# A selective scan over whole images, its input in PSUM, a multiply on GpSimd, and an output projection that moves into the next layer

## The chip, the cores and the metric

The kernel runs on one core of a Trainium2 chip. A core has four engines that matter here, each with its own queue of instructions: PE (TensorE, matrix products), DVE (VectorE, elementwise work and the scan), ACT (ScalarE, functions such as exp) and POOL (GpSimd). POOL and SP (SyncE) also issue most of the transfers between the chip's memory (DRAM) and the core's on-chip memories: SBUF, with 128 partitions, and PSUM, the small memory into which PE writes its sums. PSUM is used here as eight banks of 128 partitions x 512 floats.

The metric is the device time of one execution in microseconds (us). Everything is fp32.

## The reference

Eight images of 384 channels and 32x32 positions go through four layers. The change concerns the first and the head of the second.

Layer 0 norms an image (RMS over channels), flattens it to 1024 positions and runs a Mamba block forwards and backwards over them with the same weights; a gated 3x3 depthwise convolution is added. The core of it, for one direction:

```
u, z   = split(x_flat @ in_proj.T)                  # 384 channels each
u      = silu(causal depthwise conv of 4 taps(u))
dt,B,C = split(u @ x_proj.T)                        # 24, 16 and 16 columns
delta  = softplus(dt @ dt_proj.T + bias)            # one per channel and position
h[l]   = exp(delta[l] * A) * h[l-1] + delta[l] * u[l] * B[l]   # 16 states a channel
y[l]   = sum over the 16 states of h[l] * C[l]  + D * u[l]
out    = (y * silu(z)) @ out_proj.T
```

The layer's result is x + 0.5 * (0.25 * (out forwards + out backwards) + sigmoid(conv3x3(xn)) * xn).

Layer 1 is a 1x1 convolution, a 3x3 depthwise one and another 1x1 (with batch norms), a residual, linear attention with 8 heads, a layer norm and an MLP of 4x384 with an exact GELU. Layer 2 is a sum of seven depthwise convolutions with batch norms, which the kernel merges into one 13x13; layer 3 is a 1x1 convolution with a residual and a second 13x13 depthwise convolution with GELU.

## The kernel before

Layers 0 and 1 run together in `_layers01`, image by image; layers 2 and 3 follow when all images are through. For image b there are three strands of work, written as Python generators:

- `front(b)`, layer 0 up to the scan's inputs. It works by halves of 512 positions and by chunks of 128 channels, and leaves in DRAM delta (`dl_d`, one for each direction), delta*u (`v_d`), u of both directions added (`ud_d`), silu(z) (`z_d`), and the rows B and C (`bc_d`); x plus the local branch goes to `x1_d`. Its last step for a half is `deltas`: on DVE an add (L689), a multiply (L690) for each direction and an add of the two u, then the writes, which POOL issues.
- `scan(b)`, the scan and the output projection.
- `layer1(b)`, the second layer, which reads `x1_d`.

The main loop (L1067-1104) goes through the 48 units of scan(b). After each unit it advances the other strands, front(b+1) and layer1(b-1), so that their steps are spread over the units by their weights (90 and 310). A scheduler of the framework then fixes, at build time, the order of the instructions on each engine; so the order in which they run is near to the written one, but not the same. Buffers come from pools: a tile that has no free buffer in its pool makes the instruction that fills it wait.

A unit of the scan covers one direction d, one half h, one chunk c of 128 channels and one round r of 4 of the 16 states. The 128 partitions hold 32 channels times 4 states; the four groups j of 32 channels lie side by side, so a tile is 128 x (4 x 512). Delta and delta*u are loaded from DRAM with each channel's row given to four partitions (`dlt`, `vt`), B and C with each state's row given to 32 partitions (`bct`, two loads for each round); SP issues these. A unit is then:

- ACT: four exponentials (L775) make `da`, each with the scale -A of its partitions.
- DVE: one multiply by B over all four groups (L788) makes `du`. Then, for the unit before this one (`pend`), the multiply by C (L712), and then this unit's scan (L795 forwards, L798 backwards). One instruction scans all four groups: they are joined by one extra column each (`SEG` = 513), which restarts the recurrence with zero (a memset, L787) or with the first half's last state (`carry`, copies L785 and L802).
- PE: four matmuls (L714) with `selt`, a 128x32 matrix that sums the four states, add the product into `acc`, a PSUM bank for 128 channels x 512 positions, over the four rounds. `acc` starts as D*u through a diagonal matrix (`dgd`, direction 0) or as the forward result through the identity (direction 1).

After round 3 the forward sum is copied out by ACT (L723) and kept in `yf_d`; the backward sum is multiplied by silu(z) (`zr`) on DVE into `g` (L728). At the last chunk of a half the output projection follows at once: three output blocks of three matmuls each, `x1` is loaded again (`fr`), one DVE instruction adds (L737), and POOL issues the write to `x1_d`.

PSUM's banks: two for `acc`, three for the tag `mm` (`psum`) and three for `mo` (`long_psum`), which belongs to the MLP's long sums.

## Time and profile before

| | |
|---|---|
| device time, median of 3 runs | 5962.13 us (5957.54 to 5968.36) |
| time of the profiled execution | 5912.56 us |
| its span in the profile | 5910.8 us |
| mean granted clock of PE | 0.879 of full speed |
| busy: PE / DVE / ACT / POOL | 80% / 69% / 48% / 20% |
| matmuls / DVE instructions | 19550 / 2815 |

Where the time lies, by the start of each image's first B and C load (times in us from the start of the span, then the busy time of PE and DVE within):

| stretch | us | PE | DVE |
|---|---|---|---|
| scan of image 0 | 230-689 | 259 | 434 |
| image 1 | 689-1294 | 457 | 495 |
| image 2 | 1294-1941 | 496 | 497 |
| image 3 | 1941-2558 | 494 | 485 |
| image 4 | 2558-3114 | 478 | 491 |
| image 5 | 3114-3664 | 476 | 491 |
| image 6 | 3664-4215 | 468 | 476 |
| image 7 | 4215-4775 | 463 | 513 |
| rest of the last second layer | 4775-5050 | 235 | 23 |
| layers 2 and 3 | 5050-5911 | 809 | 136 |

How to read the profile's lines. A group of instructions is shown as line, engine, operation, output<-inputs by the program's names, partitions x elements, xcount, then the total busy time in us and the mean length of one in ns; behind the second bar stands the idle time of the engine just before them and what ended most of it. "SPq" and "POOLq" are the transfers that SP and POOL issue. A line of waits reads "PE acc L714 <- DVE du L712": PE's instruction of L714 waited for DVE's of L712; the numbers are us in total, times, and the longest. A line of the timeline gives start and length in us, engine, line, operation, tiles.

### The profile page before, as it was taken

To read this page: it belongs to the slowest core of one execution; us is meant where nothing else is said; L and a number is where in the kernel's file an instruction comes from. 1 tells how busy PE (TensorE), PEld (TensorE's weight loads), DVE (VectorE), ACT (ScalarE), POOL (GpSimd) and SP (SyncE) were. 2 spreads that over 40 slices of the span, in tenths; PEclk is the share of its full clock that TensorE was granted. 3 is DMA by queue.
4 is the path that set the end of the run, shared out by engine and by line. 5 is a ranking of instruction groups with operands and counts; after the bars stand their busy time and mean duration, and the time that the engine had idled before them with its cause. 6 is when DMAs were issued, how large, how long until landed. Compare 5 with 4: busy or idle time off the path is not lost.

```text
span 5910.8 us, 54428 instructions
## 1 busy us (share of the span) xinstructions
PE 4739.8 (80%) x19550; PEld 2105.2 (36%) x19550; DVE 4066.5 (69%) x2815; ACT 2825.7 (48%) x3934; POOL 1208.1 (20%) x2006
## 2 busy tenths in 40 slices
PE   3555557995788777978987988699878879899999
PEld 1121113331333223323332333243223324498498
DVE  0499999668955898588999899879979931011211
ACT  1544635574446635574676567557835523000211
POOL 5311121222112211221122122212210010110133
PEclk8676678997889878989998999899989979999999
DMA  8655574677546754675466457736663541366576
GB/s 278 199 171 183 169 229 153 194 202 200 188 145 187 221 184 139 168 209 161 158 209 207 149 183 199 202 124 200 178 175 114 142 102 37 86 170 161 188 168 149
DMA packets 417253, 1016.66 MB, mean 172 GB/s; under 512 B 61256, under 2 KB 111640, under 8 KB 416984
## 3 DMA queue, kind: packets, MB, share of 16 engines
q0 software_dynamic: 176576, 635.46, 37.1%
q1 hardware_dynamic: 210704, 354.31, 19.6%
q10 hardware_dynamic: 29704, 23.41, 1.5%
q8 instruction: 155, 2.54, 0.2%
q14 instruction: 114, 0.93, 0.1%
HBM read 768.58 MB, written 288.36 MB: 179 GB/s over the span
## 4 chain that ended last, share of the span: by engine, by line
PE 30%; DVE 26%; issue 21%; DMA 11%; ACT 6%; POOL 4%; SPq 1%; POOLq 0%; DVEq 0%; ACTq 0%
DVE du L798 7%; DVE du L788 7%; DVE du L795 6%; PE cv_a L316 5%; PE mo L1043 3%; DVE du L712 3%; PE in L508 3%; PE mf L508 3%; PE q L508 2%; PE acc L714 2%; DMA vr<-v_d 2%; POOL out L368 1%; ACT da L775 1%; DMA x_d<-fr 1%; PE dw L517 1%
## 5 line engine op out<-in xcount | busy, mean ns | idle before, releaser
L775 ACT ACTIVATE da<-dlt,neg_a 128x512 f32<-128x512 f32 x1536 | 1008.3, 713 | 987.3 <-DVE du L795 512.1
L788 DVE TENSOR_TENSOR du<-vr,bct 128x2048 f32<-128x2048 f32 x384 | 874.1, 2282 | 33.0 <-DMA vr<-v_d 27.1
L712 DVE TENSOR_TENSOR du<-du,bct 128x2048 f32<-128x2048 f32 x384 | 877.0, 2285 | 13.9 <-issue 10.4
L714 PE MATMUL acc<-du,selt 128*32 128x512 f32 x3072 | 596.8, 690 | 350.0 <-DVE du L712 335.1
L795 DVE TENSOR_TENSOR_SCAN du<-da,du 128x2052 f32<-128x2052 f32 x192 | 848.2, 4425 | 13.9 <-ACT da L775 10.6
L798 DVE TENSOR_TENSOR_SCAN du<-da,du 128x2052 f32<-128x2052 f32 x192 | 848.4, 4424 | 10.4 <-ACT da L775 7.2
L1043 PE MATMUL mo<-hm,w 128*128 128x512 f32 x1152 | 568.0, 635 | 84.3 <-ACT hm L1041 76.8
L508 PE MATMUL mf<-ln,w 128*128 128x512 f32 x1152 | 551.7, 618 | 24.2 <-DMA w<-w_d 22.4
L1043 PEld LDWEIGHTS mo<-hm,w 128*128 128x128 f32 x1152 | 221.4, 201 | 424.6 <-issue 254.8
L714 PEld LDWEIGHTS acc<-du,selt 128*32 128x32 f32 x3072 | 101.4, 115 | 682.2 <-DVE du L712 434.9
L508 PEld LDWEIGHTS mf<-ln,w 128*128 128x128 f32 x1152 | 215.7, 195 | 350.1 <-issue 327.4
L517 PE MATMUL dw<-dw_i,t3b 96*32 96x512 f32 x1152 | 250.1, 737 | 83.4 <-DMA dw_i<-h_d 71.5
L316 PE MATMUL cv_b<-xt_b,toep 128*64 128x256 f32 x2688 | 305.4, 389 | 14.0 <-DVE xt_b L298 14.0
L316 PE MATMUL cv_a<-xt_a,toep 128*64 128x256 f32 x2688 | 304.4, 388 | 8.8 <-DVE xt_a L298 8.8
L316 PEld LDWEIGHTS cv_b<-xt_b,toep 128*64 128x64 f32 x2688 | 282.7, 199 | 37.0 <-issue 16.7
L508 PE MATMUL in<-xn,win 128*128 128x512 f32 x576 | 291.1, 643 | 3.3 <-DVE biasf L845 2.5
L316 PEld LDWEIGHTS cv_a<-xt_a,toep 128*64 128x64 f32 x2688 | 282.5, 199 | 30.4 <-issue 10.0
L775 ACT ACT_TABLE_LOAD x213 | 273.3, 1283 | 37.0 <-DVE du L798 33.3
L517 PE MATMUL lc<-lc_i,t 96*32 96x512 f32 x1152 | 186.1, 662 | 62.3 <-DMA lc_i<-xn_d 60.1
L1041 ACT ACTIVATE hm<-mf,biasf 128x512 f32<-128x512 f32 x192 | 130.1, 687 | 197.7 <-PE mf L508 195.8
L298 DVE COPY xt_b<-xt_b 64x2480 f32<-64x2480 f32 x24 | 39.0, 1624 | 262.8 <-DMA xt_b<-xp_d 262.8
L508 PE MATMUL h<-xx,c 128*128 128x512 f32 x288 | 150.2, 681 | 67.9 <-DMA xx<-x_d 54.6
(221 smaller groups left out, 6209.3 us busy)
## 6 DMA issues: line engine op xcount, KB each, us to landing
dlt<-dl_d SPq DMA_DIRECT2D x384, 256.0 KB, 5.8
vr<-v_d SPq DMA_DIRECT2D x384, 256.0 KB, 4.9
bct<-bc_d SPq DMA_DIRECT2D x256, 256.0 KB, 4.3
ut<-u_d POOLq DMA_DIRECT2D x192, 257.5 KB, 4.6
lc_i<-xn_d POOLq DMA_DIRECT2D x192, 228.8 KB, 4.6
dw_i<-h_d POOLq DMA_DIRECT2D x192, 228.8 KB, 5.2
tp_d<-g_d POOLq DMA_DIRECT2D x64, 672.0 KB, 7.9
w<-w_d POOLq DMA_DIRECT2D x64, 576.0 KB, 5.2
```

Of the source, the lines that this page charges most:

```text
L316: nc.tensor.matmul(ps[2 * H * e : 2 * H * (e + 1), 0:BW], tp[:, 2 * (g % (GB // 2)) + e, :, :, t].rearrange("p c j -> p (c j)"), rhs, star ...
L368: nc.gpsimd.dma_start(ov[g * P : (g + 1) * P], ot.rearrange("p (b w) -> p b w", w=W))
L508: nc.tensor.matmul(ps, w[:, k, m * P : (m + 1) * P], rhs[k] if isinstance(rhs, list) else rhs[:, k, :], start=(k == 0), stop=(k == NC - 1),)
L517: nc.tensor.matmul(ps[32 * j : 32 * j + 32, :], lhs(j, i), rhs(j, i), start=(i == 0), stop=(i == taps - 1), skip_group_check=True,)
L712: nc.vector.tensor_mul(dv, dv, cct[:, 1:2, :].to_broadcast([P, 4, HALF]))
L714: nc.tensor.matmul(acc[32 * j : 32 * j + 32, :], selt, dv[:, j, :], start=False, stop=(r == NR - 1), skip_group_check=True,)
L775: nc.scalar.activation(da[:, SEG * j + 1 : SEG * (j + 1)], dlt[:, j, :], AF.Exp, scale=neg_a[:, 4 * c + j, r : r + 1],)
L788: nc.vector.tensor_mul(flat(1)[:, :, 0:HALF], vt, bct[r][:, 0:1, :].to_broadcast([P, 4, HALF]))
L795: nc.vector.tensor_tensor_scan(du[:, s], da[:, s], du[:, s], 0.0, ALU.mult, ALU.add)
L798: nc.vector.tensor_tensor_scan(du[:, s][:, ::-1], da[:, s][:, ::-1], du[:, s][:, ::-1], 0.0, ALU.mult, ALU.add)
L1041: nc.scalar.activation(hm, ps, AF.Gelu, bias=biasf[:, NC * i + f, :])
L1043: nc.tensor.matmul(acc[m], wb[:, f, m * P : (m + 1) * P], hm, start=(i == 0 and f == 0), stop=(i == FF // C - 1 and f == NC - 1),)
```

## The change

The scan goes over whole images. A unit is now one direction d, one block u of 64 channels (there are six) and one round r; its two groups j of 32 channels are tiles of their own, 128 x 1024 each, all positions in one piece. So there are still 48 units an image, with the same elements each, but no halves, no joined segments and no carry.

- The exponentials are two of 1024 in place of four of 512. The multiply by B and the scan are two each, one per group. The multiply by B writes `du` into PSUM (one buffer of two banks), the scan reads it there and writes its states `h` to SBUF (five buffers `hs`).
- The multiply by C of group 0 is made by GpSimd, right behind that group's scan; that of group 1 stays on DVE and comes, as before, behind the next unit's first multiply by B.
- PE sums as before with four matmuls of 512 a unit. `acc` holds 64 channels x 2 halves. The add of D*u is no matmul with a diagonal matrix any more: `deltas` multiplies u by D on ACT before it is written, and both directions now add through the identity (L714 of the changed kernel), behind the first round's sums.
- `yf_d` takes the forward sums in the layout of `acc`. The backward sums times silu(z) go to a new DRAM tensor `g_d` rather than to an SBUF tile.
- The output projection leaves `scan` and stands at the head of `layer1(b)`: it loads x1 and g for a half, makes the nine matmuls, and adds in place; the second layer's 1x1 convolution then reads that tile. x1 isn't written a second time. The weight of layer1 in the main loop goes from 310 to 325.
- PSUM: `acc` one bank, `du` two, `mm` two, `mo` three. The second layer's steps up to the layer norm take `mo` in place of `mm`.

In the changed kernel the exponential is L762, the multiply by B L764, the deferred multiply by C L766, the scan L769, GpSimd's multiply L773, the sums over states L708; delta's steps are L681 and L682; the loads of delta and delta*u L750, of B and C L739.

The diff, cut to its core; in `scan`, longer runs of removed lines, which stand in the listing of the kernel before, are left out:

```diff
-SEG = HALF + 1
+NU = C // 64
+N_REP, N_DA, N_HS = 6, 3, 5
...
-        accp = ctx.enter_context(tc.tile_pool(name="acc0", bufs=2, space=PSUM))
+        accp = ctx.enter_context(tc.tile_pool(name="acc0", bufs=1, space=PSUM))
...
-        yf_d = scratch([B, C, L], "yf_d")
+        yf_d = scratch([B, NU, P, HALF], "yf_d")
+        g_d = scratch([B, C, L], "g_d")
...
-        for c in range(NC):
-            nc.gpsimd.tensor_scalar_mul(dgd[:, c, :], ident, vec("D", c))
...
-            return psp.tile([P, HALF], FP, tag="mm", name=name)
+            return psp.tile([P, HALF], FP, tag="mm", name=name, bufs=2)
...
-                        nc.gpsimd.dma_start(udv[b][:, c, bass.ts(h, HALF)], ucs[0][:, c, :])
+                        ud = t2(f"ud_{b}_{h}_{c}")
+                        nc.scalar.activation(ud, ucs[0][:, c, :], AF.Copy, scale=vec("D", c))
+                        nc.gpsimd.dma_start(udv[b][:, c, bass.ts(h, HALF)], ud)
...
             pend = None
...
+            units = [(d, u, r) for d in range(2) for u in range(NU) for r in range(NR)]
+
+            def halves(t_d, u):
+
+                return bass.AP(
+                    t_d.tensor, t_d[b, 64 * u, 0].offset, [[HALF, 2], [L, 64], [1, HALF]]
+                )
             def product(un):
...
+                d, u, r, hs, acc, y0, zt = un
+                for e in range(2):
+                    for j in range(2):
+                        nc.tensor.matmul(
+                            acc[64 * e + 32 * j : 64 * e + 32 * j + 32, :], selt,
+                            hs[j][:, bass.ts(e, HALF)],
+                            start=(r == 0), stop=(r == NR - 1), skip_group_check=True,
+                        )
+                if r == 0:
                     nc.tensor.matmul(
-                        acc[32 * j : 32 * j + 32, :], selt, dv[:, j, :],
-                        start=False, stop=(r == NR - 1), skip_group_check=True,
+                        acc, ident, y0, start=False, stop=False,
+                        skip_group_check=True,
                     )
-                cols = bass.ts(h, HALF)
                 if r < NR - 1:
                     return
                 if d == 0:
-                    yt = s2(f"yt_{b}_{h}_{c}")
+                    yt = s2(f"yt_{b}_{u}")
                     nc.scalar.copy(yt, acc)
...
+                    nc.gpsimd.dma_start(yf_d[b, u], yt)
+                else:
+                    nc.vector.tensor_mul(zt, acc, zt)
+                    nc.gpsimd.dma_start(halves(g_d, u), zt)
+
+            bct = dlt = vt = acc = y0 = zt = None
+            for d, u, r in units:
+                if u == 0 and r == 0:
                     bct = []
                     for e in range(NR):
-                        t = sp.tile([P, 2, HALF], FP, tag="bct", name=f"bct_{b}_{d}_{h}_{e}", bufs=4)
+                        t = sp.tile([P, 2, L], FP, tag="bct", name=f"bct_{b}_{d}_{e}", bufs=4)
                         for o in range(2):
                             src = bass.AP(
-                                bc_d.tensor, bc_d[b, d, o * NST + 4 * e, h * HALF].offset,
-                                [[0, 32], [L, 4], [1, HALF]],
+                                bc_d.tensor, bc_d[b, d, o * NST + 4 * e, 0].offset,
+                                [[0, 32], [L, 4], [1, L]],
                             )
                             nc.sync.dma_start(t[:, o, :], src)
                         bct.append(t)
-                    if d == 1:
-                        g = a6(f"g_{b}_{h}")
                 if r == 0:
...
+                    dlt, vt = [], []
+                    for j in range(2):
+                        for src_d, to, n in ((dl_d, dlt, "dlt"), (v_d, vt, "vr")):
+                            t = sp.tile([P, L], FP, tag="rep", name=f"{n}_{b}_{d}_{u}_{j}", bufs=N_REP)
                             src = bass.AP(
-                                src_d.tensor, src_d[b, d, P * c + 32 * j, h * HALF].offset,
-                                [[L, 32], [0, 4], [1, HALF]],
+                                src_d.tensor, src_d[b, d, 64 * u + 32 * j, 0].offset,
+                                [[L, 32], [0, 4], [1, L]],
                             )
...
+                            nc.sync.dma_start(t, src)
+                            to.append(t)
+                    acc = accp.tile([P, HALF], FP, tag="acc", name=f"acc_{b}_{d}_{u}")
+                    y0 = s2(f"y0_{b}_{d}_{u}")
+                    nc.sync.dma_start(y0, halves(ud_d, u) if d == 0 else yf_d[b, u])
+                if r == 1 and d == 1:
+                    zt = s2(f"zr_{b}_{u}")
+                    nc.sync.dma_start(zt, halves(z_d, u))
+                hs = []
+                way = slice(None) if d == 0 else slice(None, None, -1)
+                for j in range(2):
+                    da = sp.tile([P, L], FP, tag="da", name=f"da_{b}_{d}_{u}_{r}_{j}", bufs=N_DA)
+                    nc.scalar.activation(da, dlt[j], AF.Exp, scale=neg_a[:, 2 * u + j, r : r + 1])
+                    du = accp.tile([P, L], FP, tag="du", name=f"du_{b}_{d}_{u}_{r}_{j}")
+                    nc.vector.tensor_mul(du, vt[j], bct[r][:, 0, :])
+                    if j == 0 and pend is not None:
+                        nc.vector.tensor_mul(pend[3][1], pend[3][1], pend_c)
+                        product(pend)
+                    h = sp.tile([P, L], FP, tag="hs", name=f"hs_{b}_{d}_{u}_{r}_{j}", bufs=N_HS)
+                    nc.vector.tensor_tensor_scan(
+                        h[:, way], da[:, way], du[:, way], 0.0, ALU.mult, ALU.add
                     )
...
+                    if j == 0:
+                        nc.gpsimd.tensor_mul(h, h, bct[r][:, 1, :])
+                    hs.append(h)
+                pend = (d, u, r, hs, acc, y0, zt)
+                pend_c = bct[r][:, 1, :]
                 yield
+            nc.vector.tensor_mul(pend[3][1], pend[3][1], pend_c)
             product(pend)
             yield
...
         def layer1(b):
             xx = []
+            w = wtile(outproj_t, f"wo_{b}")
+            for h in range(2):
+                xh, gh = a6(f"xx_{b}_{h}"), a6(f"g_{b}_{h}")
+                nc.gpsimd.dma_start(xh, x1v[b][:, :, bass.ts(h, HALF)])
+                nc.gpsimd.dma_start(gh, gv[b][:, :, bass.ts(h, HALF)])
+                xx.append(xh)
+                for m in range(NC):
+                    ps = long_psum(f"op_{b}_{m}_{h}")
+                    dense(ps, w, m, gh)
+                    o = xh[:, m, :]
+                    nc.vector.scalar_tensor_tensor(o, ps, rsm, o, ALU.mult, ALU.add)
+                    yield 3
             w = wtile(c1_d, f"c1_{b}")
             for h in range(2):
-                xh = a6(f"xx_{b}_{h}")
-                nc.gpsimd.dma_start(xh, x1v[b][:, :, bass.ts(h, HALF)])
-                xx.append(xh)
                 hh, mid = image6(f"hh_{b}_{h}")
                 for m in range(NC):
-                    ps = psum(f"h_{b}_{m}_{h}")
-                    dense(ps, w, m, xh)
+                    ps = long_psum(f"h_{b}_{m}_{h}")
+                    dense(ps, w, m, xx[h])
                     nc.scalar.activation(mid[m], rows(ps), AF.Identity, bias=bias1[:, m, :])
                     yield 3
...
-                    ps = psum(f"c2_{b}_{m}_{h}")
+                    ps = long_psum(f"c2_{b}_{m}_{h}")
...
-                work.append([layer1(b - 1), 310, 0])
+                work.append([layer1(b - 1), 325, 0])
```

## The prediction

> **What bounds the kernel now.** I read the page first (busy shares, then the 40 slices), then the groups of instructions, the waits of DVE and PE in the stretch of the scans, the busy time per engine image by image, and last the timeline of DVE. The page, busy shares and slices:
> ```profile
> PE 4739.8 (80%) x19550; PEld 2105.2 (36%) x19550; DVE 4066.5 (69%) x2815; ACT 2825.7 (48%) x3934; POOL 1208.1 (20%) x2006
> ...
> PE   3555557995788777978987988699878879899999
> ...
> DVE  0499999668955898588999899879979931011211
> ```
> The scans run from slice 2 to slice 32; behind them are one last second layer and layers 3 and 4, where DVE is idle. In the scans no engine is the bound alone: where PE shows 9, DVE often shows 5 or 6, and the other way round. The same by stretches (busy us of PE, PEld, DVE, ACT, POOL, then granted clock, DMA share, GB/s): image 4, then image 0, the first three quarters of image 1 and its last quarter:
> ```profile
> 2558.00:3114.00 556.00, 478.10 (x1722) 179.18 (x1721) 491.12 (x315) 353.19 (x477) 115.37 (x205) 0.92 0.59 181
> ...
> 230.00:690.00 460.00, 259.49 (x983) 77.71 (x986) 434.79 (x277) 260.12 (x371) 82.63 (x149) 0.67 0.53 174
> 690.00:1120.00 430.00, 299.24 (x1119) 112.77 (x1112) 393.51 (x288) 203.97 (x306) 85.90 (x149) 0.81 0.60 191
> 1120.00:1294.00 174.00, 156.93 (x484) 54.24 (x483) 100.78 (x67) 108.57 (x129) 49.63 (x79) 0.96 0.66 189
> ```
> Image 0 is DVE's (95% busy, PE 56%). The last quarter of image 1 is PE's (90%, DVE 58%): the MLP of the second layer sits there. From image 4 both are near 87%. The waits of DVE and of PE say the same (us in total, times, longest):
> ```profile
> DVE du L785 <- PE acc L714: 197.0, 37, 19.6
> ```
> ```profile
> PE acc L714 <- DVE du L712: 335.1, 78, 14.4
> ```
> DVE waits for the sums over states to free a buffer; elsewhere PE waits for DVE's multiply by C. A scan unit is these groups, and in the timeline it looks as below (start, length):
> ```profile
> L788 DVE TENSOR_TENSOR du<-vr,bct 128x2048 f32<-128x2048 f32 x384 | 874.1, 2282 | 33.0 <-DMA vr<-v_d 27.1
> L712 DVE TENSOR_TENSOR du<-du,bct 128x2048 f32<-128x2048 f32 x384 | 877.0, 2285 | 13.9 <-issue 10.4
> ...
> L795 DVE TENSOR_TENSOR_SCAN du<-da,du 128x2052 f32<-128x2052 f32 x192 | 848.2, 4425 | 13.9 <-ACT da L775 10.6
> ```
> ```profile
> 313.24 2.29 DVE L788 TENSOR_TENSOR du<-vr,bct 128x2048 f32<-128x2048 f32 x1
> 315.44 2.29 DVE L712 TENSOR_TENSOR du<-du,bct 128x2048 f32<-128x2048 f32 x1
> 317.64 4.43 DVE L795 TENSOR_TENSOR_SCAN du<-da,du 128x2052 f32<-128x2052 f32 x1
> 322.02 0.07 DVE L787 MEMSET du<- 128x4 f32 x2
> ```
> The next L788s start at 322.18, 330.93 and 339.90: (339.90-313.24)/3 = 8.89 us per unit. An instruction that doesn't need the one before it starts 0.08 us before that one's end.
>
> **The change, part by part.** *DVE in a unit.* 384 units stay (8 images of 48). A unit becomes two multiplies by B, two scans and one multiply by C, each of 1024 elements; the carry copies and memsets go. A DVE multiply of 512 takes 0.683 us (L690) and of 2048 2.283, so 150 ns are fixed and 1024 take 1.22. The scan by the same fixed part is (4425-150)/2052 = 2.08 ns per element, 2.28 us for 1024. That is 3x1.22+2x2.28 = 8.22. In the compiled order two instructions follow one they don't need (-0.16) and three follow one they do; L625 starts 0.03 us behind the end of L624, which it needs (+0.09). Result 8.15 (I use 8.16), 0.73 less than 8.89.
> An operand in PSUM: L728 and L1020 read one and take 676 and 678 ns against 683-685 from SBUF, so I take no change for scan or store; a DVE store into PSUM has no row. Bounds: 7 ns per 512 elements better, or worse by as much as ACT's rows differ between the two memories (0.68 us from PSUM, 0.71 from SBUF, 4%), 0.2 us a unit.
>
> *GpSimd's multiply*, 384 times 128x1024, has no row either. Below: POOL's memset of 882 elements takes 0.857 us, one stream, so 1.0 us. Above: its only read of SBUF, L441, takes 598 ns for 128 elements, 4.8 us if nothing of it is fixed. Two streams in and one out at the memset's rate lie between 2 and 3 us; I take 2.3, nearer the memset, whose length is the like one. [...] POOL then has 115+48x2.3 = 225 us of work in an image, under half.
> What waits behind it: POOL's queue also issues some 200 transfers an image (0.56 us each), several waiting for PE to free image buffers, so a multiply can come late, and the loads behind it too. Its result is needed by PE for one of two groups; the other group's multiply by C stands on DVE behind the next unit's first multiply, 2.4 us later, so short delays are covered. A state buffer (5 of half units) comes back about 1.5 units after, some 14 us, against about 22 us for the four du buffers of now: less slack behind PE.
> Does GpSimd's read slow DVE? In before nothing reads SBUF on POOL in the scans. Lower bound 0: beside busy ACT, PE and transfers L788 ranges only from 2261 to 2294 ns. Upper bound: every multiply holds DVE for its 2.3 us. I take 0.3 us per unit, one blocked multiply in eight, near the row. DVE unit: 8.46.
> [...]
>
> *Where it counts.* An image's 12-unit quarters are as long as the slower of DVE and PE. DVE: 12x8.89+12.7 of other work (491 less 48x9.17, by four) = 119 before, 12x8.46+12.7 = 114 after. PE: the compiled order of both kernels shows which matmuls stand between which units; I weigh them by their rows and scale an image to the measured 478 us. Before: image 1 43/102/155/164, image 2 48/97/148/188, image 3 48/97/219/117, images 4 to 6 122/109/129/117. After: image 1 81/131/145/121, image 2 85/128/128/138, image 3 85/159/93/141, image 4 85/159/114/121, images 5 and 6 131/112/114/121. The larger numbers, summed over images 1 to 6: 3182 before, about 3017 after. The real stretches are 3526, 1.11 times the first sum; so -183 us. The order matters as much as DVE's work: the MLP spreads better in images 1 to 3, worse in image 4. Images 0 and 7 are DVE's: 8 quarters by 5.2, -41. Matmul counts and PE's work are the same.
>
> *Image boundaries.* The scan of whole images needs both halves of the first layer. In the compiled order of before the second half's deltas (L689) stand 2 units into the next scan, needed 12 units in. After, for images 2 to 7, they stand between the last unit of one scan and the first of the next, which needs them by way of DRAM. SP's queue also has all of the new B and C loads ahead of the deltas. The length is seen at the start of before: deltas from 210.71 (DVE), written from 211.71, loads from 215.46, landing 5.8 us later (the median), about 11 us; then a table load and an exponential (1.28+1.25). DVE has 3 to 4 us of other work there. I take 12 us for each of 6 boundaries, +72; bounds 0 (PE has the time to catch up) and 25 (the deltas late as well).
> *Start.* The second half's first deltas are written at 264.7 now; with about 10 us of way, less some 10 that ACT gains without exponentials between them, the scan starts near 265 instead of 230. By 281 DVE has done 27 us of scan work in before; 265+27-281 = +11.
> *Out projection.* It goes through g in DRAM instead of x1: as many trips. In the last image all 18 matmuls come behind the scan instead of 9; the trace has two instructions for one (1152 of L1043 for 576), 0.49 us each by that row's busy time: 9x2x0.49 = +9. D's scaling adds 48 ACT copies (0.6 us each) and the longer exponentials save ACT 384x(4x0.63-2x1.06) = 154 us (six of 512 take 3.79 us in the timeline; 0.83 ns per element from L566's 128 and L677's 512); ACT is 63% busy, so neither counts. PSUM: one acc buffer makes the next group's first sum wait for ACT's copy or DVE's multiply, two mm buffers in place of three; the second layer's head uses the idle mo buffers. I cost it at nothing; the cover is PE's other matmuls in the quarters of DVE. Loads move the same bytes in fewer, longer pieces.
>
> Sum: -183-41+72+11+9 = -132 on the profiled execution's own 5912.56 (span 5910.8 and 1.8 around it). The median of the runs is 5962.13, 0.8% above; I take the 132 off it: 5830.
>
> **Rivals.** [...]
> *The edges eat it (no change or a little slower).* 25 us a boundary adds 78 to the sum; if the tighter buffers (14 against 22 us) leave each of 32 quarters 3 us further above its bound, 96 more: -132+174 = +42, 6004. For it: dl L689 already waits 63 us for ACT, and that wait is now in DVE's only path. Against: in images 1 to 3 PE has a backlog to work off meanwhile.
> *Everything is covered.* Nothing blocked, boundaries hidden behind PE: -211-70+20 = -261, 5701.
> *The change does nothing*, because PE holds all quarters: against it image 0 with PE at 56%.
>
> **How the numbers follow.** My forecast (5740 to 5900) 0.45; covered (below 5740) 0.22; edges (5900 to 6020) 0.18; port (above 6020) 0.15. Within 0.2% (12 us, about what three runs tell apart) I put 0.04, out of the edges' case, of which 0.03 more is faster and 0.11 slower. Range for 8 in 10: 5650 to 6060.
>
> **What would show it.** L764 and L766 at 1.22 us and L769 at 2.28; L773 near 2.3; longer L764 or L766 (a maximum far above the median) would be the port. DVE idle of 10 to 15 us at six boundaries before du L764, put down to DMA vr. First scan near 265. Image 4 longer than images 5 and 6. The forecast is wrong if a scan from PSUM is slower, or if POOL's queue makes PE wait for hs L773 in long stretches.

## The result, and the profile after

The changed kernel takes 6128.6 us (median of 4 runs, 6113.12 to 6134.38) against 5964.6 us: 1.0272 of before, 95% interval 1.0251 to 1.0294. It is slower by 2.7%; forecast were 5830 us and a range up to 6060. All ratios below are to the kernel before on the same chip in the same hours (its median there was 5902 to 5962 us). The profiled execution of before ran 0.8% below the median of its runs, so its stretches may look that much too short beside those of others.

Busy shares and two of the slices of the page, after:
```profile
PE 4903.7 (80%) x19550; PEld 2110.1 (34%) x19550; DVE 3927.8 (64%) x3007; ACT 2795.6 (46%) x3256; POOL 2363.4 (39%) x2393
...
PE   4575468886788778878988888698869769899899
...
DVE  0399986777678676867987798778788831011211
```
DVE has 139 us less to do than before (3927.8 against 4066.5), near the forecast (0.43 x 384 = 165). It idles more instead: its slices in the scans now mostly show 6 to 8 where they mostly showed 8 and 9. The groups of the scan:
```profile
L769 DVE TENSOR_TENSOR_SCAN hs<-da,du 128x1024 f32<-128x1024 f32 x768 | 1752.1, 2281 | 451.0 <-PE acc L708 384.6
L773 POOL TENSOR_TENSOR hs<-hs,bct 128x1024 f32<-128x1024 f32 x384 | 1140.4, 2971 | 1134.5 <-DVE hs L769 916.5
L764 DVE TENSOR_TENSOR du<-vr,bct 128x1024 f32<-128x1024 f32 x768 | 1083.0, 1410 | 132.7 <-DMA vr<-v_d 112.4
L708 PE MATMUL acc<-hs,selt 128*32 128x512 f32 x3072 | 796.2, 685 | 352.6 <-POOL hs L773 184.8
L766 DVE TENSOR_TENSOR hs<-hs,bct 128x1024 f32<-128x1024 f32 x376 | 470.5, 1251 | 0.0
```
The scan takes 2.28 us, as worked out, and an operand in PSUM costs it nothing (in the run with the turned order, below, 384 scans with one take 2.265 us in the mean, 384 out of SBUF 2.297). The multiply by B has a mean of 1.41 us in place of 1.22, GpSimd's one of 2.97 in place of 2.3. In front of the scans stands a new wait: 385 us for sums that have not yet freed a buffer of states. The sums themselves keep PE busy for 796 us where the same number of matmuls, as long each (685 and 690 ns), took 597. Before, the four of a unit (eight instructions, two for each) mostly ran side by side, the first of them alone in 119 of 384 units; now the first, of group 0, runs alone in 250, and the other three run later. PE's timeline, before and then after, both in image 4:
```profile
2809.54 1.06 PE L714 MATMUL acc<-du,selt 128*32 128x512 f32 x8
```
```profile
2918.32 1.04 PE L708 MATMUL acc<-hs,selt 128*32 128x512 f32 x2
...
2921.94 1.06 PE L708 MATMUL acc<-hs,selt 128*32 128x512 f32 x6
```

The waits that answer to the two shown of before (us in total, times, longest), of DVE:
```profile
DVE hs L769 <- PE acc L708: 384.6, 69, 21.0
```
and of PE:
```profile
PE acc L708 <- POOL hs L773: 184.8, 77, 8.0
PE acc L708 <- DVE hs L766: 128.3, 67, 5.8
```
PE waits for GpSimd and DVE together 313 us, where it waited 335 for DVE alone; DVE waits 385 us for PE, before 197 and, at the memset L787, 50 more. The waiting has moved to DVE's side.

Stretches image by image, from the first multiply by B of an image to that of the next (columns as in the prediction: length; busy us of PE, PEld, DVE, ACT, POOL; granted clock, DMA share, GB/s). Before, images 0 and 4:
```profile
230.00:723.00 493.00, 270.05 (x1020) 80.08 (x1020) 467.77 (x301) 272.79 (x388) 88.08 (x159) 0.67 0.54 175
...
2586.00:3142.00 556.00, 478.10 (x1722) 179.10 (x1720) 491.38 (x315) 353.18 (x477) 115.37 (x205) 0.92 0.59 182
```
The same of after:
```profile
271.00:773.00 502.00, 297.39 (x966) 80.65 (x966) 473.99 (x335) 263.24 (x286) 220.33 (x194) 0.68 0.51 164
...
2690.00:3273.00 583.00, 497.01 (x1740) 177.50 (x1738) 465.11 (x343) 343.55 (x389) 270.72 (x258) 0.91 0.56 172
```
The scan starts 41 us later and image 0 is no shorter. Image 4 takes 27 us longer, with 26 us less on DVE and 19 us more on PE. Over all images: start +41, image 0 +10, images 1 to 6 +39, -7, +21, +27, +27, +19, image 7 up to its last scan +18, the rest behind it +26. These add up to the 222 us between the two profiled executions, not to the 164 between the medians, because the one of before ran short. The granted clock of images 4 to 6 was 0.92, 0.93 and 0.91 before and 0.91, 0.93 and 0.92 after, so it doesn't explain their length.

The gaps between images are visible in DVE's timeline (after, end of image 6):
```profile
4419.55 1.22 DVE L778 TENSOR_TENSOR hs<-hs,bct 128x1024 f32<-128x1024 f32 x1
4423.01 1.31 DVE L681 TENSOR_TENSOR dl<-dl,sp 128x512 f32<-128x512 f32 x2 [2.24 <-ACT sp L676]
...
4436.44 1.23 DVE L764 TENSOR_TENSOR du<-vr,bct 128x1024 f32<-128x1024 f32 x1 [4.58 <-DMA vr<-v_d]
```
Deltas, DRAM, then the first multiply: the chain that the prediction described. From the start of an image's last unit to the next image's first multiply it is now 32 to 38 us at images 2 to 7, before 9 to 16.

### The profile page after: what moved, and what is told of

Same layout as the page of the kernel before. It is cut to its first block, busy times and chain, and to the rows that moved or that the text cites. A ratio compares the mean times of both kernels' runs of the same rounds, so it can differ in the third digit from the quotient of the medians.

```text
span 6132.6 us, 54550 instructions
## 1 busy us (share of the span) xinstructions
PE 4903.7 (80%) x19550; PEld 2110.1 (34%) x19550; DVE 3927.8 (64%) x3007; ACT 2795.6 (46%) x3256; POOL 2363.4 (39%) x2393
## 5 line engine op out<-in xcount | busy, mean ns | idle before, releaser
L769 DVE TENSOR_TENSOR_SCAN hs<-da,du 128x1024 f32<-128x1024 f32 x768 | 1752.1, 2281 | 451.0 <-PE acc L708 384.6
L773 POOL TENSOR_TENSOR hs<-hs,bct 128x1024 f32<-128x1024 f32 x384 | 1140.4, 2971 | 1134.5 <-DVE hs L769 916.5
L762 ACT ACTIVATE da<-dlt,neg_a 128x1024 f32<-128x1024 f32 x768 | 875.2, 1147 | 1174.5 <-DVE hs L769 1118.0
L764 DVE TENSOR_TENSOR du<-vr,bct 128x1024 f32<-128x1024 f32 x768 | 1083.0, 1410 | 132.7 <-DMA vr<-v_d 112.4
L708 PE MATMUL acc<-hs,selt 128*32 128x512 f32 x3072 | 796.2, 685 | 352.6 <-POOL hs L773 184.8
L766 DVE TENSOR_TENSOR hs<-hs,bct 128x1024 f32<-128x1024 f32 x376 | 470.5, 1251 | 0.0
L708 PEld LDWEIGHTS acc<-hs,selt 128*32 128x32 f32 x3072 | 121.7, 116 | 814.6 <-POOL hs L773 299.8
L500 PE MATMUL op<-g,wo 128*128 128x512 f32 x288 | 156.8, 691 | 148.0 <-issue 54.5
L509 PE MATMUL lc<-lc_i,t 96*32 96x512 f32 x1152 | 202.6, 666 | 61.1 <-DMA lc_i<-xn_d 57.2
L509 PE MATMUL c<-ut,t 128*32 128x512 f32 x768 | 186.7, 680 | 71.8 <-DMA ut<-u_d 59.1
```

What stands on the lines that cost most here:

```text
L500: nc.tensor.matmul(ps, w[:, k, m * P : (m + 1) * P], rhs[k] if isinstance(rhs, list) else rhs[:, k, :], start=(k == 0), stop=(k == NC - 1),)
L509: nc.tensor.matmul(ps[32 * j : 32 * j + 32, :], lhs(j, i), rhs(j, i), start=(i == 0), stop=(i == taps - 1), skip_group_check=True,)
L708: nc.tensor.matmul(acc[64 * e + 32 * j : 64 * e + 32 * j + 32, :], selt, hs[j][:, bass.ts(e, HALF)], start=(r == 0), stop=(r == NR - 1), s ...
L762: nc.scalar.activation(da, dlt[j], AF.Exp, scale=neg_a[:, 2 * u + j, r : r + 1])
L764: nc.vector.tensor_mul(du, vt[j], bct[r][:, 0, :])
L766: nc.vector.tensor_mul(pend[3][1], pend[3][1], pend_c)
```

## The experiments

Four theories at first. A: the edges between images cost what is seen there. B: the few buffers of states do. C: GpSimd's multiply does, by holding DVE and by being late. D: the split sums do. Later came G (POOL's queue, where a multiply that waits for a scan keeps transfers back) and H (in images 1 to 6 PE sets the pace, so DVE's time is worth little there).

**Edges.**
```diff
-                work.append([front(b + 1), 90, 0])
+                work.append([front(b + 1), 130, 0])
```


> The changed kernel with the weight of front(b+1) in the main loop at 130 in place of 90, so that the last deltas of the next image stand 10 or more units ahead of the image's end on DVE, not behind its last unit. Theory A (edges): of the changed kernel's loss, some 145 us come from the gaps between images, 32 to 38 us from the start of an image's last unit to the first multiply of the next one where before has 9 to 16. Then these gaps fall to 9 to 15 us and the time falls by 120 to 160 us, to about 5970 to 6010. Theory B (buffers: DVE waits for the sums to free a buffer of hs): the gaps close but DVE then waits inside the image for what PE has not done, and no more than 50 us are gained. Theory C (GpSimd holds DVE at SBUF): as B.

6255.9 us, 1.0494 (1.0478 to 1.0511). The gaps did close, to 9.4 us at all six boundaries behind images 1 to 6, and the images got longer by more than that: image 4 is 601 us in place of 583, its inside 592 in place of 551. So the gap was no cost to be added up: what DVE doesn't wait at the edge it waits inside. That front's work, moved ahead, stands in the way of the second layer's would explain the loss; it is not shown. Theory A falls; B's and C's expectation of a gain up to 50 was wrong too.

**One buffer of states more or fewer** (`hs`; the space comes from `t2`, tiles of 512 positions that the first and the second layer use, or from `rep`, the loads of delta and delta*u).
```diff
-N_A6, N_T2, N_S2, N_W, N_IM = 7, 11, 3, 4, 6
-N_REP, N_DA, N_HS = 6, 3, 5
+N_A6, N_T2, N_S2, N_W, N_IM = 7, 10, 3, 4, 6
+N_REP, N_DA, N_HS = 6, 3, 6
```


> The changed kernel with six buffers hs in place of five and, for the space, ten t2 in place of eleven. Theory B (buffers): DVE's wait for the sums before a scan, 385 us in the changed kernel, falls below 250, and the time falls by 60 to 130 us. Theory A (edges) and theory C (GpSimd holds DVE): the time stays within 25 us.

6173.3 us, 1.0353 (1.0338 to 1.0369): slower. DVE's wait for the sums fell to 339 us, while delta's wait for ACT rose from 151 to 278. Three more runs took this apart. Four `hs`:
```diff
-N_REP, N_DA, N_HS = 6, 3, 5
+N_REP, N_DA, N_HS = 6, 3, 4
```

> The changed kernel with four buffers hs in place of five, and nothing else. It asks what this buffer's slack is worth without another pool being touched. Theory B (buffers: the scans' wait for the sums, 385 us, is a cost of its own): the wait grows well past 450 us and the time by 60 us or more. Theory H (PE paces images 1 to 6, and a scan that waits for PE only shows that): DVE waits elsewhere or longer at no cost, and the time stays within 30 us of the changed kernel's, ratio to before 1.022 to 1.033.

6172.7 us, 1.0354 (1.0336 to 1.0373), with the wait at 431 us. Ten `t2`, five `hs`:
```diff
-N_A6, N_T2, N_S2, N_W, N_IM = 7, 11, 3, 4, 6
+N_A6, N_T2, N_S2, N_W, N_IM = 7, 10, 3, 4, 6
```

> The changed kernel with ten buffers t2 in place of eleven, and nothing else. It takes apart the run with six hs and ten t2, which came out at 1.035 of before where the changed kernel has 1.027. Theory B (hs buffers have a price of their own): the tenth t2 alone costs more than the sixth hs gives back, so this run comes out above 1.035, with delta's steps waiting for ACT. If a sixth hs gives nothing, this run comes out at 1.035 like the other, or, if t2 doesn't matter either and the order of the work alone moved, at 1.022 to 1.033.

6121.1 us, 1.0289 (1.0273 to 1.0304). Six `hs`, five `rep`:
```diff
-N_REP, N_DA, N_HS = 6, 3, 5
+N_REP, N_DA, N_HS = 5, 3, 6
```

> The changed kernel with six buffers hs in place of five and, for the space, five rep (the loads of delta and delta*u) in place of six. With four hs it came out at 1.035, with five at 1.027. Theory B: the sixth gives about what the fifth gave, 1.018 to 1.024, unless the loads come late, which DVE's wait for vr (112 us with six rep) shows. Theory H (PE paces; from five on the slack is enough): 1.022 to 1.033.

6140.0 us, 1.0322 (1.0305 to 1.0339). The fifth buffer is worth 0.8%, between what B and H expected; a sixth gives nothing, with either pool reduced for it. Ten `t2` alone don't explain the 1.0353, and what does stays open. The 385 us of the new wait are no price to be added up either: with six `hs` and five `rep` they fall to 284, and the kernel is no faster.

**Without GpSimd, in two ways.** Group 0's multiply on DVE, in the same place:
```diff
-                        nc.gpsimd.tensor_mul(h, h, bct[r][:, 1, :])
+                        nc.vector.tensor_mul(h, h, bct[r][:, 1, :])
```


> The changed kernel with group 0's multiply by C on DVE, at the same place, in place of GpSimd. DVE's unit gets 1.22 us more and loses what GpSimd held it (200 us in all, 0.5 us a unit): 9.4 in place of 8.7. If DVE's work sets the quarters, +0.7 x 384 = +270 at most, and +100 where PE, buffers and edges set most of them. If GpSimd's lateness cost PE and DVE more than its work saved (theory C at its strongest), the time stays or falls.

6099.9 us, 1.0230 (1.0215 to 1.0245): faster than with GpSimd, by about 0.4%, though DVE has 224 us more to do (4152.0 against 3927.8). And with no engine making it:
```diff
-                    if j == 0:
-                        nc.gpsimd.tensor_mul(h, h, bct[r][:, 1, :])
```

> The changed kernel without group 0's multiply by C on any engine: this part of the computation is left out. Nothing on GpSimd reads SBUF in the scans any more. Theory C (GpSimd holds DVE): multiplies by B go back to 1.23 us at most 1.3, DVE's busy time falls by about 190 us, PE waits no more for GpSimd (185 us), and the time falls by 100 to 200 us. Theory A (edges) or B (buffers): the gaps between images and the waits for a buffer stay, and the time falls by less than 50 us.

5952.2 us, 0.9989 (0.9979 to 0.9998). The groups of this kernel:
```profile
PE 4893.2 (82%) x19550; PEld 2096.8 (35%) x19550; DVE 3725.1 (63%) x3007; ACT 2777.1 (47%) x3241; POOL 1229.2 (21%) x2009
...
L764 DVE TENSOR_TENSOR du<-vr,bct 128x1024 f32<-128x1024 f32 x768 | 945.2, 1231 | 100.5 <-DMA vr<-v_d 80.4
```
The multiply by B is back at 1.231 us and DVE's busy time is 203 us lower, with the same instructions on DVE. So GpSimd's multiply held DVE for 0.53 us a unit, and its whole price is 1.0272 - 0.9989 = 2.8%, about 169 us: as much as the change lost. PE's busy time hardly changes (4893.2 against 4903.7), and the sums still take 817 us of it, with the multiply on DVE 866: what splits them is the new layout, whose two groups are ready at different times, and not GpSimd. The gaps behind images 1 and 2 are 129 and 126 us here, and these images are no longer for it (630 and 636 us, in the changed kernel 639 and 636). The other half of the finding is as important: with this multiply for nothing and 341 us less on DVE than before (4066.5 less 3725.1, 0.89 us a unit), the new layout is just level with before.

**What of GpSimd's multiply costs.** Cut to 64 positions, in its place in the queue:
```diff
-                        nc.gpsimd.tensor_mul(h, h, bct[r][:, 1, :])
+                        nc.gpsimd.tensor_mul(h[:, 0:64], h[:, 0:64], bct[r][:, 1, 0:64])
```


> The changed kernel with GpSimd's multiply by C cut to the first 64 of 1024 positions; the other 960 of group 0 are left out of the computation. POOL's queue keeps the instruction, its place and its wait for the scan; only its length goes, from 2.3 us or more to a few tenths. Theory C (the multiply's length: it holds DVE at SBUF and makes the sums late): the time falls by 130 to 180 us, to the 0.999 of before that the kernel without this multiply had. Theory G (POOL's queue: transfers for PE stand behind a multiply that waits for the scan): the wait stays, so the ratio to before stays between 1.015 and 1.027.

5996.6 us, 1.0064 (1.0042 to 1.0085). The instruction still takes 0.97 us in the mean, not a few tenths, but DVE is no longer held: its busy time is 3725.5 us, that of the run without the multiply 3725.1. The length is 2.1%, some 124 us; 0.75%, some 45 us, remain with a short instruction that waits for the scan in POOL's queue. C is most of it. The rest may be G or the late result, for which PE still waits 76 us; the runs don't tell these apart. Then the whole multiply, but laid beside a scan:
```diff
-                    nc.vector.tensor_mul(du, vt[j], bct[r][:, 0, :])
-                    if j == 0 and pend is not None:
...
-                    nc.vector.tensor_tensor_scan(
-                        h[:, way], da[:, way], du[:, way], 0.0, ALU.mult, ALU.add
-                    )
-                    if j == 0:
-                        nc.gpsimd.tensor_mul(h, h, bct[r][:, 1, :])
...
+                nc.vector.tensor_mul(h0, vt[0], bct[r][:, 0, :])
+                du = accp.tile([P, L], FP, tag="du", name=f"du_{b}_{d}_{u}_{r}")
+                nc.vector.tensor_mul(du, vt[1], bct[r][:, 0, :])
+                if pend is not None:
+                    nc.vector.tensor_mul(pend[3][1], pend[3][1], pend_c)
+                    product(pend)
+                nc.vector.tensor_tensor_scan(
+                    h0[:, way], das[0][:, way], h0[:, way], 0.0, ALU.mult, ALU.add
+                )
+                nc.gpsimd.tensor_mul(h0, h0, bct[r][:, 1, :])
...
+                nc.vector.tensor_tensor_scan(
+                    h1[:, way], das[1][:, way], du[:, way], 0.0, ALU.mult, ALU.add
+                )
```


> The changed kernel with DVE's order in a unit turned so that both multiplies by B and the deferred multiply by C come first and the two scans last, group 0's from SBUF and in place, group 1's from PSUM behind it. Then GpSimd's multiply of group 0 (2.33 us unhindered) falls beside group 1's scan (2.28 us), which reads PSUM. Nothing is left out. Theory C in its form 'GpSimd and DVE's multiplies hold each other': DVE's held time, some 200 us in all, goes to under 60, GpSimd's multiply goes from a median of 3.31 to 2.4 us, and the time falls by 60 to 170 us (ratio to before 0.998 to 1.017). Theory G (POOL's queue) or a cost of GpSimd's lateness alone: the holding goes, the time stays within 25 us of the changed kernel.

6033.9 us, 1.0129 (1.0104 to 1.0154), half of the loss gone. GpSimd's group here:
```profile
L774 POOL TENSOR_TENSOR hs<-hs,bct 128x1024 f32<-128x1024 f32 x384 | 953.2, 2483 | 1165.2 <-DVE hs L771 975.9 <-issue 129.3 <-PE acc L708 20.5
```
Its median is 2.36 us (after: 3.31) and the mean 2.48. DVE's busy time is 3830.8, so 106 us of holding remain against 203, not under 60: where the multiply starts late it runs beside the next unit's multiplies (the first of them takes 1.44 us in the mean). The ones of the changed kernel that collide are easily found in the two timelines. DVE:
```profile
504.65 1.23 DVE L764 TENSOR_TENSOR du<-vr,bct 128x1024 f32<-128x1024 f32 x1
505.80 2.84 DVE L681 TENSOR_TENSOR dl<-dl,sp 128x512 f32<-128x512 f32 x1
...
513.61 2.27 DVE L769 TENSOR_TENSOR_SCAN hs<-da,du 128x1024 f32<-128x1024 f32 x1
515.81 0.66 DVE L681 TENSOR_TENSOR dl<-dl,sp 128x512 f32<-128x512 f32 x1
516.39 3.37 DVE L764 TENSOR_TENSOR du<-vr,bct 128x1024 f32<-128x1024 f32 x1
```
and POOL:
```profile
504.76 3.32 POOL L773 TENSOR_TENSOR hs<-hs,bct 128x1024 f32<-128x1024 f32 x1 [4.96 <-DVE hs L769]
...
516.03 2.65 POOL L773 TENSOR_TENSOR hs<-hs,bct 128x1024 f32<-128x1024 f32 x1 [3.76 <-issue]
```
At 516.03 GpSimd comes first, and the 1.22 us multiply of DVE ends 1.1 us behind GpSimd's end (518.68): 3.37 us. At 504.76 DVE's multiply (504.65 to 505.88) is first, and GpSimd, started beside it, takes 3.32 us, 1 us more than its 2.33, about what that multiply still had to run; DVE's next instruction (L681, 0.66 us at 515.81) takes 2.84 and ends 0.56 us behind GpSimd's end (508.08). The scans of the kernel with the turned order are a control: those of its group 1, with one operand in PSUM, never took more than 2.29 us, while three of group 0's, with both in SBUF, took 4.42 to 4.71, each beside a multiply of GpSimd's.

**Split sums.**
```diff
-                    for j in range(2):
+                    for j in (1, 0):
                         nc.tensor.matmul(
```


> The changed kernel with the order of the sums over states turned round: the matmuls of group 1 (whose multiply by C on DVE ends last) come first on PE, those of group 0 behind them. In the changed kernel the first sum of group 0 waits for GpSimd and runs alone, and the other three follow a second wait; the sums take 796 us of PE's time where the same 3072 matmuls of the same mean length (685 and 690 ns) took 597 before, four side by side. Theory D (split sums): the sums fall back to 600 to 680 us of PE's time, PE's wait for GpSimd mostly goes, and the time falls by 60 to 150 us. Theories A (edges), B (buffers), C (GpSimd holds DVE): within 25 us.

6084.8 us on a faster chip, 1.0310 (1.0295 to 1.0326). The sums:
```profile
L708 PE MATMUL acc<-hs,selt 128*32 128x512 f32 x3072 | 684.4, 697 | 438.7 <-DVE hs L766 353.7 <-DVE zr L725 45.9 <-ACT yt L722 25.5
```
112 us less of PE, and nothing gained: part of the time that the first sum ran alone is now waited for (PE waits 354 us for DVE's multiply, where it waited 313 for GpSimd and DVE). In images 4 and 5 PE's busy time hardly moved (490 and 489 us, 497 and 493 in the changed kernel). Theory D falls.

**Parts of the change, alone, in the kernel before.** The PSUM pools:
```diff
-        accp = ctx.enter_context(tc.tile_pool(name="acc0", bufs=2, space=PSUM))
+        accp = ctx.enter_context(tc.tile_pool(name="acc0", bufs=1, space=PSUM))
...
-            return psp.tile([P, HALF], FP, tag="mm", name=name)
+            return psp.tile([P, HALF], FP, tag="mm", name=name, bufs=2)
...
-                    ps = psum(f"h_{b}_{m}_{h}")
+                    ps = long_psum(f"h_{b}_{m}_{h}")
...
```

> The kernel before with the changed kernel's PSUM pools alone: one acc buffer, two mm, and the second layer's steps up to the layer norm on mo. Two banks stay idle. Theory E (the smaller pools hold PE up): 40 to 120 us slower than before, with waits of PE for ACT's copy or DVE's multiply of acc. Otherwise, as the prediction had it, within 20 us of before.

5916.9 us, 1.0019 (1.0006 to 1.0033). The output projection, in `layer1` as in the changed kernel (there with `psum`), and in `scan`:
```diff
-                nc.vector.tensor_mul(g[:, c, :], acc, zt)
...
+                nc.vector.tensor_mul(zt, acc, zt)
+                nc.gpsimd.dma_start(gv[b][:, c, cols], zt)
...
```

> The kernel before with the output projection alone moved to the head of the second layer, g going through DRAM, weight 325. Theory F (the move costs in itself, because PE waits at the head for g, written and loaded by POOL's queue; 53 us of such waits in the changed kernel): 30 to 80 us slower than before. As the prediction had it, +9 in the tail and otherwise nothing: within 20 us.

5887.9 us, 0.9975 (0.9964 to 0.9986). Neither costs what E or F supposed; the move even gains a quarter of a per cent.

**What DVE's time is worth in the kernel before.**
```diff
-                nc.vector.tensor_mul(dv, dv, cct[:, 1:2, :].to_broadcast([P, 4, HALF]))
+                nc.vector.tensor_mul(dv[:, 0:2, :], dv[:, 0:2, :], cct[:, 1:2, :].to_broadcast([P, 2, HALF]))
```


> The kernel before with its multiply by C on two of the four groups only; the other two are left out of the computation. DVE's unit falls by 1.07 us, to 7.8, and nothing else changes, so this prices DVE's time in the kernel before. The prediction's way (an image's quarters are as long as the slower of DVE and PE): -104 in images 0 and 7, -129 in images 1 to 6, about -230. Theory H (PE paces images 1 to 6; it waits for DVE's products 132, 64, 62, 56, 0, 0, 0 and 17 us in images 0 to 7): -50 in image 0, -17 in image 7, at most -20 to -30 in each of images 1 to 3 and nothing in images 4 to 6, about -130 to -150, and images 4 to 6 as long as before within 5 us each.

5859.5 us, 0.9833 (0.9805 to 0.9861): 98 us for 395 us of DVE's busy time (4066.5 less 3671.5). Images 0 and 4:
```profile
234.00:677.00 443.00, 262.38 (x1019) 81.75 (x1019) 416.40 (x301) 277.77 (x391) 87.74 (x158) 0.68 0.59 194
...
2547.00:3102.00 555.00, 478.89 (x1720) 176.31 (x1719) 441.26 (x314) 348.93 (x473) 115.12 (x205) 0.93 0.60 181
```
Image 0 gives back all of its 50 us. Image 4 has 50 us less of DVE and is 555 us long, before 556; images 5 and 6 lose 4 and 9. Image 1 is 24 us longer, images 2 and 3 are 9 shorter each. This is H; its 98 us are less than the 130 to 150 expected because images 1 to 3 gave nothing. (The two profiled executions differ by 50 us only, the one of before having run short; a 0.8% on its stretches would add 4 to 5 us to each image, so the gains in images 5 and 6 may be some 9 and 14.) The profile before had said so, in a view that the prediction took as one sum over all images: PE's waits by stretch. Images 4 to 6, the longest waits:
```profile
PE dw L517 <- DMA dw_i<-h_d: 48.7, 17, 12.5
PE mo L1043 <- ACT hm L1041: 45.0, 24, 3.7
PE ms_b L570 <- ACT ms_r L567: 23.9, 6, 7.2
```
The wait for DVE's multiply by C doesn't occur there. Of its 335 us, 132 lie in image 0, 182 in images 1 to 3, 17 in image 7. In images 4 to 6 PE is idle for 73 to 83 us each, and only 8 to 12 of them are for DVE, 35 to 47 for ACT and 19 to 30 for transfers.

**A version that is a little faster than both.** The output projection moved as above, and the first layer one image further ahead, to use PE's idle half of image 0:
```diff
-            if b + 1 < B:
-                work.append([front(b + 1), 90, 0])
+            if b == 0:
+                work.append([ahead(1, 2), 180, 0])
+            elif b + 2 < B:
+                work.append([ahead(b + 2), 90, 0])
...
```


> The kernel before with the output projection at the head of the second layer (as in the run of that alone, 0.9975 of before) and the first layer of the images one image further ahead: image 0, where DVE paces and PE idles for nearly half the time, carries front(1) and front(2), images 1 to 5 carry front(b+2), image 6 carries none. Theory H (PE paces images 1 to 6, DVE images 0 and 7): image 0 gets 20 to 45 us longer by DVE's work on the second front, image 6 loses a front's matmuls and gets 40 to 70 us shorter, the images between stay; 0.985 to 0.997 of before. If PE's work is not what paces image 6, nothing is gained there and the ratio is 1.000 to 1.006.

5941.7 us, 0.9966 (0.9954 to 0.9978). Image 0 went from 492 to 553 us, more than expected; image 6 from 566 to 532, less than expected, with 65 us less of PE's work (482.8 to 417.6). The gain is no more than the projection's move gives alone (0.9975, intervals overlap), but both versions are faster than the two kernels of this case, by about 0.3%.

## Why the prediction was wrong

*The step that failed* is "an image's 12-unit quarters are as long as the slower of DVE and PE", with the -183 that it gave for images 1 to 6; measured were +127 (3663 against 3536 us; +98 if before's stretches are 0.8% too short). It let every quarter in which DVE's row was the larger shrink with DVE's work, and it took PE's 335 us of waits for DVE as spread over the scans. By its own numbers DVE's row was the larger in 13 of the 24 quarters of before, so the lighter DVE made 13 x 5.2 x 1.11 = 75 of the 183, and the new order of PE's matmuls the other 108. Both failed. By the run with half of the multiply by C, DVE's time was worth 0.25 us per us (98/395), about half of it in image 0. In the new layout it was 0.34 (1.0230 less 0.9989, 144 us, for the 427 us between 4152.0 and 3725.1). At 0.25 to 0.34 the 165 us of the forecast unit are worth 41 to 56 us, not 75 + 41. The better spread of the MLP gave nothing that the runs show: without GpSimd's multiply, in the new order and with a DVE lighter by 0.89 us a unit, images 1 to 6 take 3549 us, before 3536 (3565 with the 0.8%). What is shown in place of the rule is that DVE hardly sets the length of images 1 to 6; that PE does, with its waits for ACT and transfers, rests on its idle times and on image 6 of the last run.

*DVE's unit.* That DVE's whole saving came out near the forecast is luck in part: without GpSimd's multiply DVE's work fell by 0.89 us a unit and not by 0.73, and the holding took back 0.53 and not 0.3.

*GpSimd.* The length was right (2.3 forecast, 2.33 to 2.36 unhindered). The holding was sized at 0.3 us a unit and measured 0.53. The mis-sizing of 88 us is the smaller part; the error of kind is that its price was reckoned as DVE's time alone. The multiply cost 169 us in all, 0.83 us for each of the 203 that it held DVE, while at 0.25 to 0.34 the holding would have cost 51 to 69. In image 0, which is DVE's, price and holding are alike: without the multiply DVE has 54 us less to do there, and the image is 53 us shorter. Of the rest, 45 us stay where nothing holds DVE (the multiply cut to 64 positions). The chance put on "port" (0.15) was for such a holding, and the sign named for it came: the longest L764 took 7.45 us, where the median is 1.23. That the two engines share a port no run shows; what the runs show is the holding in the two timelines above, 768 scans with an operand in PSUM, none above 2.29 us, and three scans out of SBUF at 4.42 to 4.71 us.

*Boundaries*: the mechanism was there, at some 24 us and not 12 more than before, near the upper bound; but adding it up was wrong. The run with the earlier front closed the gaps and lost 2.2% more.

*Start*: the first multiply came at 271 (265 forecast). Where nothing else disturbs (the run without the multiply), the end of image 0 shows the start's net cost: 269 + 449 = 718, against 722 before less 0.89 x 48 = 43 of DVE's work, so +39 and not +11. *Tail*: 1167 us behind the last scan against 1141; the run with half the multiply in the old layout has 1157, so +10 to +26 where +9 was forecast.

*PE's work* "the same": the matmuls are, their time isn't: PE's busy time rose by 164 us, 199 more in the sums less small changes elsewhere. The forecast costed PE at nothing; the turned order, which took 112 us of it back and gained nothing, speaks for that. *PSUM pools and projection* at nothing: right (+0.2% and -0.25%).

Put together in the runs' own terms: GpSimd's multiply +169; DVE's lighter unit about -85 (an estimate: 341 us without holding, at 0.25; at 0.34 it is -116); the layout's start, end and the rest +78 (or +109), which is what is left to reach +162. Of this rest the profiles show 35 us of later start (269 against 234 us in the two runs with a light DVE) and 10 to 26 us of tail; why images 4 to 6 together take 20 us more in the new layout than in the old one with a light DVE stays open.

Also open is how GpSimd's multiply lengthens images in which PE hardly waits for it: in images 1 to 6 the changed kernel's PE waits 8 to 28 us an image for GpSimd, and image 4 is 23 us longer than without the multiply. Over the whole span PE waits as long for its products without it (259 us for DVE's multiply and 48 for the scan) as with it (313). That a late result passes on through ACT's and DMA's turns is possible, not shown.

## What to carry to other kernels

Before a saving on an engine is counted, read by stretch who waits for that engine: a sum over the span hides that the waits lie in half of the eight images and that one of them gives back half of what can be had, and the cheapest test is to leave some of that engine's work out and see what the time gives back. A multiply moved to GpSimd beside DVE can cost more than it takes off DVE: here it lengthened the kernel by 169 us, 25 us more than the same multiply on DVE. It comes late (PE waited 185 us for it), stands in a queue with transfers, and wants to be laid beside work of DVE that it was not seen to hold: beside a scan with an operand in PSUM half of the loss was gone (1.0129 in place of 1.0272). A gap that appears in one engine's timeline need not be a cost: closing six gaps of 32 to 38 us made this kernel slower.

## What the runs showed of the hardware

GpSimd's multiply of 128x1024 fp32 takes 2.33 us unhindered (the shortest of 384). Where it and a DVE multiply out of SBUF (1.22 us) ran side by side, one of the two got longer: DVE's took 3.37 us and ended 1.1 us behind GpSimd's, or GpSimd's took 3.32. One of DVE's (at 1729.49, beside two multiplies of GpSimd's in a row) took 7.45 us. DVE's scan reading one operand from PSUM takes 2.28 us, in 768 of them never more than 2.29. A DVE multiply that writes to PSUM takes hardly longer than one to SBUF (1.231 and 1.217 us with GpSimd quiet). Matmuls of 32 columns each, 690 ns long, keep PE busy for 597 us for 3072 when the first goes ahead alone in 119 of 384 groups of four, and for 796 when it does in 250; in the timelines shown, two, six and eight of their instructions took 1.04, 1.06 and 1.06 us together.
